# An MLP's two layers by Strassen's product in blocks of 256 pixels, inside a four-layer fp32 kernel

## The chip, the cores and the metric

One core of a Trainium2 chip; everything is fp32. The time is the device time of one execution in microseconds; one core, so it is that core's. A run quoted here is the median of its executions, with the lowest and highest in brackets.

## The reference, cut to what matters

Four image layers follow each other: a deformable attention with an MLP (layer 0), then three attention layers. Only the MLP at the end of layer 0 is changed. With B x H x W = 2 x 32 x 32 = 2048 pixels and C = 512 channels:

```python
xn2 = _bn(x, bn2_g, bn2_b)
h1 = jax.nn.gelu(jnp.einsum('bchw,oc->bohw', xn2, mlp_w1) + mlp_b1[None, :, None, None], approximate=False)
return x + jnp.einsum('bchw,oc->bohw', h1, mlp_w2) + mlp_b2[None, :, None, None]
# mlp_w1: 2048 x 512, mlp_w2: 512 x 2048
```

## The kernel before: the parts that matter

`w1` (4 chunks of 128 input channels x 2048 outputs) and `w2` (16 chunks x 512) lie in SBUF. A half image of 512 pixels is a block; `P` is 128, `CC` 4, `HID` 2048, `HALF` 512. `norm` is a generator that computes the next layer's group norm step by step between the MLP's groups.

```python
xn = normed(0, 0)
for b in range(B):
    for half in range(2):
        ...
        h1 = one.tile([P, HID // P, HALF], F32, name="hid")
        for m in range(HID // P):
            ph = ps.tile([P, HALF], F32, name="ph")
            for k in range(CC):
                nc.tensor.matmul(                                   # L991: first layer
                    ph, w1[:, k, m * P : (m + 1) * P], xn_now[:, k, :], start=(k == 0), stop=(k == CC - 1)
                )
            nc.scalar.activation(h1[:, m, :], ph, AF.Gelu, bias=col("mlp_b1", m))
            if b == 1 and m % 4 == 3:
                advance(norm)
        if (b, half) == (B - 1, 1):
            qkv1, proj1 = load_w(wa, "wa", [a["qkv1_w"], a["proj1_w"]])
        for m in range(CC):
            pp = ps.tile([P, HALF], F32, name="pp2")
            for k in range(HID // P):
                nc.tensor.matmul(                                   # L1002: second layer
                    pp, w2[:, k, m * P : (m + 1) * P], h1[:, k, :], start=(k == 0), stop=(k == HID // P - 1)
                )
            nc.vector.scalar_tensor_tensor(
                xs[b][:, m, n], pp, col("mlp_b2", m), xs[b][:, m, n], ALU.add, ALU.add
            )
            nc.sync.dma_start(out=x_d[b, m, :, n], in_=xs[b][:, m, n])
```

## Time and profile before

| | before |
|---|---|
| time, us | 3727.63 (3726.69 to 3728.03, the first 3 runs) |
| TensorE busy | 99% of 3725.8 us |
| MLP, first matmul to the next layer's first | 440.2 us (12%) |
| VectorE busy in one pair of MLP layers (110 us) | 2.8 us |
| pitch of a matmul record of 512 columns | 429.1 ns |

How to read it: TensorE (PE) works without a gap through the MLP, so the MLP's time is the number of its matmul records times their pitch, the time from one record's start to the next one's. A record is half of one fp32 matmul of the program. The lines behind the table are shown in the prediction below.

### The profile page before, as it was taken

To read this page: it belongs to the slowest core of one execution; us is meant where nothing else is said; L and a number is where in the kernel's file an instruction comes from. 1 tells how busy PE (TensorE), PEld (TensorE's weight loads), DVE (VectorE), ACT (ScalarE), POOL (GpSimd) and SP (SyncE) were. 2 spreads that over 40 slices of the span, in tenths; PEclk is the share of its full clock that TensorE was granted. 3 is DMA by queue.
4 is the path that set the end of the run, shared out by engine and by line. 5 is a ranking of instruction groups with operands and counts; after the bars stand their busy time and mean duration, and the time that the engine had idled before them with its cause. 6 is when DMAs were issued, how large, how long until landed. Compare 5 with 4: busy or idle time off the path is not lost.

```text
span 3725.8 us, 37390 instructions
## 1 busy us (share of the span) xinstructions
PE 3675.3 (99%) x15234; PEld 1342.1 (36%) x15234; DVE 2371.8 (64%) x2317; ACT 1586.4 (43%) x1940; POOL 478.6 (13%) x188
## 2 busy tenths in 40 slices
PE   9999999999999999999999999999999999999999
PEld 4333333333333333333333334444433333444443
DVE  6988998998996998998998960000036447030222
ACT  4655566565664566656656541100134234111111
POOL 1112122122121012121132210000001000000000
PEclk9999999999999999999999999999999999999999
DMA  4100012001010110010101001000100000000000
GB/s 149 24 15 14 18 24 62 17 20 18 18 23 12 13 23 18 18 24 12 24 18 22 18 2 51 9 34 12 57 1 1 1 1 0 14 0 0 6 29 24
DMA packets 96852, 78.42 MB, mean 21 GB/s; under 512 B 10656, under 2 KB 84768, under 8 KB 95904
## 3 DMA queue, kind: packets, MB, share of 16 engines
q1 hardware_dynamic: 96528, 75.41, 8.3%
q8 instruction: 123, 2.02, 0.2%
q14 instruction: 57, 0.47, 0.0%
q10 hardware_dynamic: 144, 0.52, 0.0%
HBM read 64.12 MB, written 10.75 MB: 20 GB/s over the span
## 4 chain that ended last, share of the span: by engine, by line
PE 93%; DVE 3%; ACT 3%; issue 0%; DMA 0%; POOL 0%; SPq 0%; DVEq 0%; POOLq 0%; ACTq 0%
PE z L443 44%; PE sim L465 6%; PE pw L135 6%; PE ph L991 6%; PE pp L1002 6%; PE pm L1026 5%; PE pmv L135 4%; PE score L1130 3%; PE score L135 3%; PE pv L1178 3%; PE ppr L1057 2%; PE pp L549 1%; ACT h L451 1%; DVE h L425 1%; DVE h L456 1%; PE pf L135 1%
## 5 line engine op out<-in xcount | busy, mean ns | idle before, releaser
L443 PE MATMUL z<-h,cpb_w 128*64 128x512 f32 x8192 | 1788.7, 594 | 28.5 <-ACT h L451 26.6
L451 ACT ACTIVATE h<-z,b2h 128x1024 f32<-128x1024 f32 x1024 | 1137.8, 1114 | 868.0 <-PE z L443 858.7
L425 DVE CUSTOM_DVE_ANT_1 h<-tab,tab 128x1024 f32<-128x1024 f32 x1024 | 1221.8, 1234 | 121.1 <-PE z L443 120.7
L443 PEld LDWEIGHTS z<-h,cpb_w 128*64 128x64 f32 x8192 | 575.6, 137 | 1208.9 <-issue 1107.5
L456 DVE SCALAR_TENSOR_TENSOR h<-h,turn,h 128x1024 f32<-128x1024 f32 x512 | 689.6, 1347 | 5.3 <-ACT h L451 5.3
L410 POOL TENSOR_SCALAR tab<-tab,pc 128x512 f32<-128x512 f32 x63 | 270.9, 4300 | 1576.3 <-DMA tab<-slog_d 1116.3
L1005 DVE SCALAR_TENSOR_TENSOR x<-pp,pc,x 128x512 f32<-128x512 f32 x16 | 12.0, 749 | 375.8 <-PE pp L1002 375.8
L465 PE MATMUL sim<-h,w 128*32 128x512 f32 x2048 | 234.3, 595 | 0.7 <-DVE h L456 0.7
L135 PE MATMUL pw<-p,vT 128*128 128x512 f32 x512 | 221.8, 593 | 1.3 <-DVE y L1236 1.3
L991 PE MATMUL ph<-xn,wa 128*128 128x512 f32 x512 | 220.9, 593 | 1.4 <-POOL xn L975 1.4
L1002 PE MATMUL pp<-hid,wb 128*128 128x512 f32 x512 | 220.4, 592 | 0.0
L1131 ACT ACTIVATE p<-score 128x1024 f32<-128x1024 f32 x144 | 139.5, 1021 | 156.8 <-PE score L1130 156.8
L1068 DVE TENSOR_TENSOR acc<-acc,p 128x2048 f32<-128x2048 f32 x56 | 129.6, 2315 | 105.1 <-ACT p L1131 57.8
L994 ACT ACTIVATE hid<-ph,pc 128x512 f32<-128x512 f32 x64 | 44.0, 687 | 332.6 <-PE ph L991 332.6
L953 POOL TENSOR_SCALAR hc<-x,sc,sh 128x1024 f32<-128x1024 f32 x16 | 29.0, 1822 | 902.3 <-DVE sh L949 870.1
L1070 DVE TENSOR_TENSOR acc<-p 128x2048 f32<-128x2048 f32 x12 | 27.5, 2291 | 182.2 <-ACT p L1265 108.8
L991 PEld LDWEIGHTS ph<-xn,wa 128*128 128x128 f32 x512 | 97.1, 190 | 123.2 <-issue 120.4
L1002 PEld LDWEIGHTS pp<-hid,wb 128*128 128x128 f32 x512 | 97.4, 190 | 122.4 <-issue 122.4
L135 PEld LDWEIGHTS pw<-p,vT 128*128 128x128 f32 x512 | 97.1, 190 | 122.5 <-issue 120.9
L411 POOL TENSOR_SCALAR tab<-tab,pc 128x512 f32<-128x512 f32 x63 | 131.1, 2081 | 16.3 <-DMA tab<-slog_d 16.2
L1130 PE MATMUL score<-q,k 64*128 64x512 f32 x512 | 127.2, 615 | 0.0
L1026 PE MATMUL pm<-hc,wa 128*64 128x512 f32 x512 | 122.5, 604 | 0.0
(217 smaller groups left out, 2044.5 us busy)
## 6 DMA issues: line engine op xcount, KB each, us to landing
tab<-slog_d SPq DMA_DIRECT2D x128, 256.0 KB, 6.3
wa<-in_qkv_w SPq DMA_DIRECT2D x8, 768.0 KB, 6.8
xt<-in_xt SPq DMA_DIRECT2D x8, 512.0 KB, 3.8
wa<-in_mlp_w SPq DMA_DIRECT2D x4, 1024.0 KB, 17.0
wb<-in_mlp_w SPq DMA_DIRECT2D x16, 256.0 KB, 5.4
x_d<-x SPq DMA_DIRECT2D x16, 256.0 KB, 2.0
out<-x SPq DMA_DIRECT2D x16, 256.0 KB, 2.0
wa<-in_proj_w SPq DMA_DIRECT2D x8, 256.0 KB, 9.0
```

The costliest lines, as they stand in the source:

```text
L135: nc.tensor.matmul(pm, w, m, start=(k == 0), stop=(k == len(pairs) - 1))
L410: engine.tensor_scalar(tabs[0], tabs[0], col("cpb_w1", 0), col("cpb_b1"), ALU.mult, ALU.add)
L425: nc.vector._custom_dve(TENSOR_ADD_SAT, out=h1, in0=tx[:, quad, ri, :].unsqueeze(1).to_broadcast([P, H, W]), in1=ty[:, quad, ri, :].unsque ...
L443: nc.tensor.matmul(z[point * 64 : point * 64 + 64, n], cpb_w2[:, part * 64 : part * 64 + 64], h1s[point][:, n], start=True, stop=True,)
L451: nc.scalar.activation(h2, z, AF.Relu, bias=b2h[:, part : part + 1])
L456: nc.vector.scalar_tensor_tensor(parts[0], parts[0], turn, parts[1], ALU.mult, ALU.add)
L465: nc.tensor.matmul(sim[quad * 32 : quad * 32 + 32, n], w3[:, lo : lo + 32], h2[:, n], start=(r == 0 and j < 4), stop=False,)
L991: nc.tensor.matmul(ph, w1[:, k, m * P : (m + 1) * P], xn_now[:, k, :], start=(k == 0), stop=(k == CC - 1))
L1002: nc.tensor.matmul(pp, w2[:, k, m * P : (m + 1) * P], h1[:, k, :], start=(k == 0), stop=(k == HID // P - 1))
L1026: nc.tensor.matmul(pm[at : at + wide], w[:, k, lo + at : lo + at + wide], h[k][:, n], start=(k == 0), stop=(k == CC - 1),)
L1130: nc.tensor.matmul(sc[:, part, :], ks[part][r, left[part]], qs[part][r, n], start=True, stop=True)
L1131: nc.scalar.activation(p[:, :, n], sc, AF.Exp, scale=scale)
```

## The change

The intent: TensorE is the bound and VectorE idle in the MLP, so multiply less and add more. Each layer's weights and pixels are split into halves; Strassen's scheme (in Winograd's form) gets the product of two 2 x 2 arrays of blocks from seven products instead of eight. The blocks are now 256 pixels, so a product streams 128 pixels. The sums on the weights' side are formed once, on VectorE, while block 0 is computed in the plain way; those on the pixels' side are formed for each block, and the seven products are combined on VectorE (with ScalarE copying product 1 out of PSUM). Condensed:

```diff
+            def lefts(w, name):                     # sums of the weights, once
...
+                def form(engine, cols):
+                    engine.tensor_tensor(t1[c], a21[c], a22[c], ALU.add)
+                    engine.tensor_tensor(t2[c], t1[c], a11[c], ALU.subtract)
+                    engine.tensor_tensor(a21[c], a11[c], a21[c], ALU.subtract)
+                    engine.tensor_tensor(t4[c], a12[c], t2[c], ALU.subtract)
+                return (a11, a12, t4, a22, t1, t2, a21), form
+            def rights(v, name):                    # the same for the pixels, by chunk (L1006 to L1009)
...
+            def products(left, right, cols, some, pms=None):
+                a, b = pms                          # two PSUM tiles, "pma" and "pmb", of 4 x 128 columns
+                at = {1: a[:, 0], 2: a[:, 1], 6: a[:, 2], 3: a[:, 3], 4: b[:, 0], 5: b[:, 1], 7: b[:, 2]}
+                for i in some:
+                    product(at[i], i, left, right, cols)
+            def combined(pms, p1, lower):
...
+                nc.vector.tensor_tensor(upper, a[:, 1:3], twice(p1), ALU.add)              # L1036
+                nc.vector.tensor_tensor(u, b[:, 1:3], twice(upper[:, 1]), ALU.add)         # L1037
+                nc.vector.tensor_tensor(lower, b[:, 0:2], twice(u[:, 1]), ALU.add)         # L1038
+                nc.vector.tensor_tensor(upper[:, 1], a[:, 3], u[:, 0], ALU.add)            # L1039
...
+            for blk in range(1, NBLK):
+                for c in range(MC + 1):             # MC = 8 groups of first-layer outputs
+                    if c < MC:
+                        pms = products(left1, right1, slice(c * P, (c + 1) * P), (1, 2, 6, 7, 5, 4, 3))
+                        p1 = first_of(pms)          # nc.scalar.copy, L1044
+                    if c:
+                        activated(c - 1, upper)     # Gelu of the lower half L1095, of the upper L1096
+                    if c < MC:
+                        upper = combined(pms, p1, hid[:, MC + c, :].rearrange("p (j n) -> p j n", j=2))
+                    if c:
+                        form_right2(slice(c - 1, c))
+                    if b == 1 and c % 4 == 3:
+                        advance(norm)
...
+                cols = [slice(c * P, (c + 1) * P) for c in range(2)]
+                both = [products(left2, right2, cols[c], (1, 2)) for c in range(2)]
+                for c in range(2):
+                    products(left2, right2, cols[c], (6, 7, 5, 4, 3), both[c])
+                    lower = two.tile([P, 2, PX], F32, name="lower")
+                    upper = combined(both[c], first_of(both[c]), lower)
+                    added(blk, 2 + c, lower.rearrange("p j n -> p (j n)"))
+                    added(blk, c, upper)
```

To make room, weights of a later layer (`g2`, `v2`, `vbias`) are loaded after the MLP instead of in its middle, and a buffer ring of that layer is split in two.

More of the change, by code (lines that the diff above doesn't have):

```diff
@@ L884, in general, with layers @@
             attend([(k[:DH], q[:DH])], 1.0, vT, [(m * P, P) for m in range(CC)], store)
-    def layers(f, g2, v2, t2_b, o2_b):
+    def layers(f, fold_d, t2_b, o2_b):
         f.enter_context(in_order(tc))
@@ L891, in layers @@
         keep = f.enter_context(tc.tile_pool(name="keep", bufs=1))
-        chan = f.enter_context(tc.tile_pool(name="chan", bufs=9))
+        chan = f.enter_context(tc.tile_pool(name="chan", bufs=4))
         ps_m = f.enter_context(tc.tile_pool(name="ps_m", bufs=2, space=PSUM))
@@ L898, in layers @@
             nc.sync.dma_start(out=vb, in_=a["vb"].rearrange("l (k p) -> p l k", p=P))
-        vbias = keep.tile([P, C], F32, name="vbias")
-        nc.sync.dma_start(out=vbias, in_=a["vb"][0].partition_broadcast(P))
         gb3 = keep.tile([P, CC], F32, name="gb3")
@@ L969, in layers, with blocks @@
             ps = mlp.enter_context(tc.tile_pool(name="mlp_ps", bufs=3, space=PSUM))
-            def normed(b, half):
-                n = slice(half * HALF, (half + 1) * HALF)
-                xn = two.tile([P, CC, HALF], F32, name="xn2")
+            BLK = 256
+            PX = BLK // 2
+            def blocks(v, k, n):
+                return [
+                    [v[:, i * k // 2 : (i + 1) * k // 2, j * n // 2 : (j + 1) * n // 2] for j in range(2)]
+                    for i in range(2)
+                ]
@@ new lines, in lefts @@
+            def lefts(w, name):
+                k, n = w.shape[1:]
+                (a11, a21), (a12, a22) = blocks(w, k, n)
+                t1, t2, t4 = [one.tile([P, k // 2, n // 2], F32, name=f"{name}s{i}") for i in (1, 2, 4)]
+                def form(engine, cols):
+                    c = (slice(None), slice(None), cols)
+                    engine.tensor_tensor(t1[c], a21[c], a22[c], ALU.add)
[3 more added lines that the diff above has]
+                return (a11, a12, t4, a22, t1, t2, a21), form
@@ new lines, in rights, with form @@
+            def rights(v, name):
+                k, n = v.shape[1:]
+                (b11, b12), (b21, b22) = blocks(v, k, n)
+                t1, t2, t4 = [one.tile([P, k // 2, n // 2], F32, name=f"{name}t{i}") for i in (1, 2, 4)]
+                def form(chunks):
+                    c = (slice(None), chunks, slice(None))
+                    nc.vector.tensor_tensor(t1[c], b12[c], b11[c], ALU.subtract)
+                    nc.vector.tensor_tensor(t2[c], b22[c], t1[c], ALU.subtract)
+                    nc.vector.tensor_tensor(b12[c], b22[c], b12[c], ALU.subtract)
+                    nc.vector.tensor_tensor(t4[c], b21[c], t2[c], ALU.subtract)
+                return (b11, b21, b22, t4, t1, t2, b12), form
@@ new lines, in product @@
+            def product(pm, i, left, right, cols):
+                l, r = left[i - 1], right[i - 1]
+                accumulate(pm, [(l[:, k, cols], r[:, k, :]) for k in range(l.shape[1])])
+            def products(left, right, cols, some, pms=None):
+                if pms is None:
+                    pms = [ps.tile([P, 4, PX], F32, name=f"pm{i}") for i in "ab"]
+                a, b = pms
+                at = {1: a[:, 0], 2: a[:, 1], 6: a[:, 2], 3: a[:, 3], 4: b[:, 0], 5: b[:, 1], 7: b[:, 2]}
+                for i in some:
+                    product(at[i], i, left, right, cols)
+                return pms
@@ new lines, in combined, with twice @@
+            def combined(pms, p1, lower):
+                a, b = pms
+                upper = two.tile([P, 2, PX], F32, name="upper")
+                u = two.tile([P, 2, PX], F32, name="u")
+                def twice(v):
+                    return v.unsqueeze(1).to_broadcast([P, 2, PX])
+                nc.vector.tensor_tensor(upper, a[:, 1:3], twice(p1), ALU.add)
+                nc.vector.tensor_tensor(u, b[:, 1:3], twice(upper[:, 1]), ALU.add)
+                nc.vector.tensor_tensor(lower, b[:, 0:2], twice(u[:, 1]), ALU.add)
+                nc.vector.tensor_tensor(upper[:, 1], a[:, 3], u[:, 0], ALU.add)
+                return upper.rearrange("p j n -> p (j n)")
@@ L974, in normed, with first_of @@
+            def first_of(pms):
+                p1 = two.tile([P, PX], F32, name="p1")
+                nc.scalar.copy(p1, pms[0][:, 0])
+                return p1
+            left1, form1 = lefts(w1, "w1")
+            left2, form2 = lefts(w2, "w2")
+            def normed(blk):
+                b, n = blk * BLK // HW, slice(blk * BLK % HW, blk * BLK % HW + BLK)
+                xn = one.tile([P, CC, BLK], F32, name="xn2")
                 for cc in range(CC):
@@ L978, in normed @@
                 return xn
-            xn = normed(0, 0)
-            for b in range(B):
-                for half in range(2):
-                    n = slice(half * HALF, (half + 1) * HALF)
-                    xn_now = xn
-                    if (b, half) != (B - 1, 1):
-                        xn = normed(*divmod(2 * b + half + 1, 2))
-                    h1 = one.tile([P, HID // P, HALF], F32, name="hid")
-                    for m in range(HID // P):
-                        ph = ps.tile([P, HALF], F32, name="ph")
-                        for k in range(CC):
-                            nc.tensor.matmul(
-                                ph, w1[:, k, m * P : (m + 1) * P], xn_now[:, k, :], start=(k == 0), stop=(k == CC - 1)
-                            )
-                        nc.scalar.activation(h1[:, m, :], ph, AF.Gelu, bias=col("mlp_b1", m))
-                        if b == 1 and m % 4 == 3:
-                            advance(norm)
-                    if (b, half) == (B - 1, 1):
-                        qkv1, proj1 = load_w(wa, "wa", [a["qkv1_w"], a["proj1_w"]])
-                    for m in range(CC):
-                        pp = ps.tile([P, HALF], F32, name="pp2")
-                        for k in range(HID // P):
-                            nc.tensor.matmul(
-                                pp, w2[:, k, m * P : (m + 1) * P], h1[:, k, :], start=(k == 0), stop=(k == HID // P - 1)
-                            )
-                        nc.vector.scalar_tensor_tensor(
-                            xs[b][:, m, n], pp, col("mlp_b2", m), xs[b][:, m, n], ALU.add, ALU.add
-                        )
-                        nc.sync.dma_start(out=x_d[b, m, :, n], in_=xs[b][:, m, n])
-                if b == 0:
-                    for w, j in ((g2, 0), (v2, 1)):
-                        nc.sync.dma_start(out=w, in_=fold_d[j])
@@ new lines, in normed_rights, with added @@
+            def normed_rights(blk):
+                right, form = rights(normed(blk), "xn")
+                form(slice(0, CC // 2))
+                return right
+            NBLK = B * HW // BLK
+            MC = HID // P // 2
+            def added(blk, m, src):
+                b, at = blk * BLK // HW, blk * BLK % HW
+                x = xs[b][:, m, at : at + BLK]
+                nc.vector.scalar_tensor_tensor(x, src, col("mlp_b2", m), x, ALU.add, ALU.add)
+                nc.sync.dma_start(out=x_d[b, m, :, at : at + BLK], in_=x)
@@ new lines, in layers @@
+            xn = normed(0)
+            hid = one.tile([P, HID // P, BLK], F32, name="hid")
+            for c in range(MC):
+                for m in (MC + c, c):
+                    pm = ps.tile([P, BLK], F32, name="pmp", tag="pma")
+                    accumulate(pm, [(w1[:, k, m * P : (m + 1) * P], xn[:, k, :]) for k in range(CC)])
+                    nc.scalar.activation(hid[:, m, :], pm, AF.Gelu, bias=col("mlp_b1", m))
+                form1(nc.vector, slice(c * P, (c + 1) * P))
+            right1 = normed_rights(1)
@@ new lines, in layers, with activated @@
+            for m in (2, 3, 0, 1):
+                pm = ps.tile([P, BLK], F32, name="pmp2", tag="pmb")
+                accumulate(pm, [(w2[:, k, m * P : (m + 1) * P], hid[:, k, :]) for k in range(HID // P)])
+                added(0, m, pm)
+                if m >= 2:
+                    form2(nc.vector, slice((m - 2) * P, (m - 1) * P))
+            for blk in range(1, NBLK):
+                b = blk * BLK // HW
+                hid = one.tile([P, HID // P, BLK], F32, name="hid")
+                right2, form_right2 = rights(hid, "hid")
+                def activated(c, upper):
+                    nc.scalar.activation(hid[:, MC + c, :], hid[:, MC + c, :], AF.Gelu, bias=col("mlp_b1", MC + c))
+                    nc.scalar.activation(hid[:, c, :], upper, AF.Gelu, bias=col("mlp_b1", c))
+                upper = None
+                for c in range(MC + 1):
[10 more added lines that the diff above has]
+                        advance(norm)
+                if blk + 1 < NBLK:
+                    right1 = normed_rights(blk + 1)
+                else:
+                    qkv1, proj1 = load_w(wa, "wa", [a["qkv1_w"], a["proj1_w"]])
+                cols = [slice(c * P, (c + 1) * P) for c in range(2)]
[6 more added lines that the diff above has]
+                    added(blk, c, upper)
@@ L1104, in layers @@
         wb_stack.close()
+        fold2 = f.enter_context(tc.tile_pool(name="fold2", bufs=1))
+        vbias = fold2.tile([P, C], F32, name="vbias")
+        nc.sync.dma_start(out=vbias, in_=a["vb"][0].partition_broadcast(P))
+        g2, v2 = [fold2.tile([P, CC, C], F32, name=name) for name in ("g2", "v2")]
+        for w, j in ((g2, 0), (v2, 1)):
+            nc.sync.dma_start(out=w, in_=fold_d[j])
+        outs = f.enter_context(tc.tile_pool(name="outs", bufs=5))
         vp = f.enter_context(tc.tile_pool(name="vp", bufs=1))
@@ L1191, in layers @@
                 if ls == 7:
-                    o = chan.tile([P, HW], F32, name="o", tag="chan")
+                    o = outs.tile([P, HW], F32, name="o")
                     nc.vector.tensor_copy(o, pv)
@@ L1328 @@
         w1 = layer0(l0, fold_d, t2_b, o2_b)
-    with tc.tile_pool(name="fold2", bufs=1) as pool, ExitStack() as fast:
-        g2, v2 = [pool.tile([P, CC, C], F32, name=name) for name in ("g2", "v2")]
-        layers(fast, g2, v2, t2_b, o2_b)
+    with ExitStack() as fast:
+        layers(fast, fold_d, t2_b, o2_b)
     bad = nc.values_load(flag[0:1, 0:1], min_val=0, max_val=P)
```

## The prediction

> **What bounds the kernel now.** I read the page first: TensorE (PE) is busy for 99% of the span at a granted clock of 0.9 or more in every slice, and the chain that ended last is 93% PE. So only what shortens PE's own work, or makes PE wait, can move the time.
>
> ```profile
> span 3725.8 us, 37390 instructions
> PE 3675.3 (99%) x15234; PEld 1342.1 (36%) x15234; DVE 2371.8 (64%) x2317; ACT 1586.4 (43%) x1940; POOL 478.6 (13%) x188
> PEclk9999999999999999999999999999999999999999
> PE 93%; DVE 3%; ACT 3%; issue 0%; DMA 0%; POOL 0%; SPq 0%; DVEq 0%; POOLq 0%; ACTq 0%
> ```
>
> Then the chain in order of time, from 2240 us on (start, length, what). The MLP is these eight stretches without a gap, alternating first layer (L991) and second (L1002).
>
> ```profile
> 2246.53 0.78 POOL xn L975
> 2247.31 0.35 issue
> 2247.66 55.17 PE ph L991 x128
> 2302.84 54.93 PE pp L1002 x128
> ...
> 2632.88 54.93 PE pp L1002 x128
> 2687.82 13.88 PE pm L1026 x64
> ```
>
> The MLP therefore takes 2687.82 - 2247.66 = 440.2 us, 12% of the span. One fp32 matmul of the program leaves two records (64 matmuls, 128 records), and 54.93/128 = 429.1 ns is the pitch of one record of 512 columns. The 592 ns that the groups show is a latency; records overlap, so I count pitches only.
>
> The busy time of each engine in the stretches of the first half block's two layers (us, PE, PEld, DVE, ACT, POOL) shows how empty the others are:
>
> ```profile
> 2247.70:2302.80 55.10, 55.10 (x129) 24.51 (x130) 0.57 (x1) 11.59 (x16) 4.84 (x7) 1.00 0.24 81
> 2302.80:2357.80 55.00, 55.00 (x130) 24.41 (x129) 2.25 (x3) 0.69 (x1) 3.01 (x4) 1.00 0.04 15
> ```
>
> VectorE (DVE) has room here, and the change spends it. The groups that price the new, smaller instructions are these (line, operation, shapes, count, busy, mean ns):
>
> ```profile
> L135 PE MATMUL pk<-wy,xt 128*128 128x128 f32 x128 | 16.4, 282 | 0.0
> L518 PE MATMUL pa<-cst,at 128*128 128x128 f32 x64 | 8.7, 279 | 0.0
> L252 DVE TENSOR_TENSOR cpb_w<-cpb_w,pw 128x128 f32<-128x128 f32 x1 | 0.3, 279 | 0.0
> L1044 DVE TENSOR_TENSOR vT<-pmv,vbias 128x512 f32<-128x512 f32 x16 | 11.1, 691 | 62.1 <-PE pmv L135 62.1
> L1068 DVE TENSOR_TENSOR acc<-acc,p 128x2048 f32<-128x2048 f32 x56 | 129.6, 2315 | 105.1 <-ACT p L1131 57.8 <-ACT p L1265 45.8
> L994 ACT ACTIVATE hid<-ph,pc 128x512 f32<-128x512 f32 x64 | 44.0, 687 | 332.6 <-PE ph L991 332.6
> L389 ACT COPY vbd<-pkv 128x128 f32<-128x128 f32 x8 | 2.2, 275 | 0.0
> L939 ACT ACT_TABLE_LOAD x4 | 5.1, 1283 | 0.1
> ```
>
> The decisive one is pk: 128-column fp32 matmuls with fresh 128x128 weights each, exactly the new kind. Its 16 records take 2.05 us from first start to last end; the first lasts 377 ns, some 100 ns more than the usual 275 because its weight load is exposed. So the pitch is (2.05 - 0.10 - 0.275)/15 = 111.7 ns; I use 111.5. All eight bursts look alike. The weight load (190 ns a record) stays hidden at this pitch.
>
> **What the Trainium skill says.** "TensorE: Matmul & The Clock Gate", Back-to-back issue gap and the part on 53.3 ns: a warm pitch of N/2.4 + 2.5 ns. The trace agrees at 512 columns if a record is two passes: 2x512/2.4 + 2.5 = 429.2 against 429.1. At 128 it would give 109.2; the transposes pa do that (8 records in 0.87 us of the chain), pk is at 111.5, and the measured pk decides. "VectorE: DVE Perf Modes", Mode 2x_2P: fp32 tensor_tensor stays at one element a cycle of 0.96 GHz, 1.04 ns a column; the trace agrees (2315 - 691)/1536 = 1.06. "SBUF — State Buffer", Who interferes with whom: VectorE and GpSimd share a port pair under a lock; the trace agrees in that one L425 instruction takes 3394 ns against a median of 1217 beside GpSimd work. In the MLP GpSimd has only a few short operations at block boundaries. I book nothing for it.
>
> **The change part by part.**
>
> Removed: all eight stretches, 440.2 us. Now there are eight blocks of 256 pixels, the first plain, seven by Strassen.
>
> Block 0, plain: 128 matmuls of 256 columns, 256 records at 2x256/2.4 + 2.5 = 215.8 ns (an estimate between the two measured widths) = 55.2 us, as much as half of an old pair. VectorE forms sums of the weights beside it: 8x4 operations of 256 columns and 2x4 of 1024. From the rows, an operation costs about 145 + 1.05 ns a column: 128 columns 279, 256 413, 1024 1220. That is 13.2 + 9.8 = 23 us under 55, each behind a matmul that has read the old block; hidden. w2 lands about 15 us after the MLP starts (transfer view) and is first needed at 27.
>
> Blocks 1 to 7: a layer was 64 matmuls of 256 columns; it is now 112 of 128 columns (8 groups x 7 products x 2 chunks, or 2 x 7 x 8), seven eighths of the column work. A block has 224 matmuls, 448 records x 111.5 = 49.95 us, where a plain one has 55.0. Seven: 349.7 us. PE work is then 404.9, 35.3 us less than now. The ideal 7/8 would save 48 us; the fixed cost of short matmuls takes the rest.
>
> Is VectorE fast enough? A group of the first layer lasts 28 x 111.5 = 3.12 us on PE. VectorE does three additions of 256 columns, one of 128, then four of 128 to form the second layer's right sides: 3x413 + 5x279 = 2.63 us, plus some 35 ns for each of about six dependent steps = 2.85 us, 91% of the group. ScalarE: one copy 0.27, two Gelus of 256 columns at about 0.47 (687 less 256 x 0.84) = 1.2 us. Both fit, barely for VectorE, and three PSUM buffers of each kind let PE run ahead. So PE still bounds within the layer.
>
> Where PE waits: between the layers. In the built program the copy of the first product waits for the last matmul of its group, so the whole combination starts when the group ends. Take the moment S at which PE would begin the second layer; the last group's results are there at S + 0.165 (275 less 111). Copy done S + 0.48; three additions with gaps S + 0.51, 0.96, 1.40 to 1.82; last addition to 2.10; Gelu of the lower half 1.85 to 2.32; of the upper to 2.83. PE's first product needs that upper half in its eighth chunk, at S + 14 x 0.1115 = 1.55. It waits **1.3 us** a block, 9.1 us for seven. The formed sums are needed only after four products (7.1 us) and are there by S + 4.
>
> In blocks 4 to 7 the next layer's norm is interleaved. Each of the first four steps puts 1.54 us (two statistics, one aggregate) on VectorE; with 0.3 us of slack a group, some 0.3 us is left at the boundary in three blocks, 1 us. The step with Ln and Exp costs two table loads of 1.28 us during which VectorE waits: about 3.3 us of delay in group 3 of the last block, 2.4 left at the boundary. Together 3.4 us.
>
> After the MLP: qkv1's weights (4 MB) are now loaded under 25 us instead of 55; they took about 11.5 us at 390 GB/s in the transfer view. g2, v2 and vbias load after the MLP; vbias has 14 us, the others hundreds. Fewer chan buffers delay the second norm's outputs, but by the built program's waits the first two are free one projection step (5.5 us) before they are read. I book 0.
>
> Sum: 404.9 + 9.1 + 3.4 = 417.4 us against 440.2: **22.8 us less**, 3727.6 - 22.8 = 3704.8, so 3705 us, 0.6% faster.
>
> **The rivals.**
> (A) VectorE becomes the bound in the first layer. At 3.4 us a group instead of 2.85 it would add (3.4 - 3.12) x 8 x 7 = 16 us: 3720. For it: 91% load, small operations, semaphores both ways with ScalarE. Against it: the op prices come from like operations, and the row with a PSUM operand (691 ns at 512 columns) lies on the same line as the one without (2315 at 2048).
> (B) The long stream of short matmuls runs slower than the bursts of 16: fetching or weight loading shows only over hundreds of records. At 122.8 ns all PE gain is gone (55.0/448), and the time would be about 3740. Against it: in the timeline, one-column matmuls with full weights (pb) run at about 101 ns a record (8 in 0.81 us), so weight loading is not quite at its limit.
> (C) PE reaches the 109.2 ns of the transposes and the boundaries overlap better (0.5 us): 3136 x 2.3 ns = 7.2 and 5.6 less: 3692.
> (D) A late load or buffer after the MLP stalls PE, 5 to 10 us: 3713. The margins above speak against it.
>
> **Range and chances.** Pitch uncertainty (109 to 113.5) is -8 to +6 us; boundaries 0.5 to 3 us each, -6 to +12; VectorE as in A. I take 3692 to 3720 for eight times in ten. Two per cent faster would need 3653, more than the ideal saving with no wait at all (48 us); two per cent slower 3802, which only a pitch over 140 ns gives.
>
> **What would show it.** In the changed kernel: 128-column matmul records 3136 in the MLP, pitch 111.5 inside a group; the MLP from first matmul to L1138's first in 417 us; a gap of about 1.3 us on PE released by ScalarE's Gelu (L1096) once a block, and no large gaps released by VectorE; VectorE near 90% busy in first-layer windows and a third in the second; time after the MLP unchanged at about 1038 us. It is wrong if the pitch differs, if PE waits for VectorE in every group, or if the stretch after the MLP grows.

## The result, and the profile after

| | before | changed |
|---|---|---|
| time, us | 3727.4 (3726.69 to 3728.03, 4 runs) | 3706.11 (3705.36 to 3712.39, 4 runs) |
| ratio | | 0.9947 [0.9929, 0.9964] |
| MLP, first matmul to the next layer's first | 440.2 | 417.4 |
| from there to the end | 1037.98 | 1038.21 |

A ratio is the mean time of one kernel's fast runs over that of the other's of the same rounds, so not quite the ratio of the medians quoted. The change is 21.3 us faster; predicted were 22.8 and 3705 us.

The profiled execution is the slowest of the four, 3712.39 us. Its excess lies outside the change: its MLP begins at 2254.89 us, where before it began at 2247.66. These 7.2 us are there by 220 us after the start, in code that the change doesn't touch. A later run of the same kernel (e9) has the MLP begin at 2248.9 and last 417.4 us again. I compare the MLP's duration from here on, since the start differs by up to 7 us from run to run.

The traces show what goes with that difference: the clock that TensorE was granted in the first 90 us. The two windows, of the kernel before and of the changed one (the number after POOL's busy time is the granted clock):

```profile
20.00:90.00 70.00, 66.24 (x252) 27.90 (x252) 49.23 (x83) 26.63 (x29) 7.39 (x5) 0.98 0.38 110
20.00:90.00 70.00, 64.67 (x222) 29.04 (x222) 43.30 (x77) 22.19 (x26) 5.61 (x3) 0.90 0.36 104
```

The thirteen traces fall into four groups by this clock: at 0.98 the MLP begins at 2247.7 to 2248.2 us, at 0.95 at 2248.8 to 2249.2, at 0.93 at 2251.6 to 2251.8, and at 0.90 at 2254.9. Why the clock differs there from run to run is not known.

The page of the changed kernel (busy us, share, instructions; then VectorE's busy tenths in 40 slices):

```profile
span 3710.5 us, 43026 instructions
PE 3649.9 (98%) x17602; PEld 1550.3 (42%) x17602; DVE 2557.3 (69%) x2905; ACT 1615.8 (44%) x2074; POOL 488.7 (13%) x204
DVE  5988998998996898998998873455346447030222
```

PE is busy for 25.4 us less with 2368 records more: shorter records, closer together. VectorE has taken up the work of seven products, and the MLP's slices (the 25th to the 29th) no longer show zeros.

The chain of the changed kernel in order of time, through block 0, one border between layers, the start of the second layers of two blocks in a row, and the last one (start, length, what):

```profile
2254.89 55.49 PE pmp L135 x256
...
2334.95 0.46 PE pma L135 x4
...
2335.49 0.28 ACT p L1044
...
2335.78 0.44 DVE upper L1036
...
2336.24 0.43 DVE u L1037
...
2336.70 0.43 DVE hid L1038
...
2337.16 0.51 ACT hid L1095
2337.67 0.41 ACT hid L1096
...
2338.12 7.63 PE pma L135 x66
2345.75 5.36 PE pmb L135 x48
...
2389.57 7.63 PE pma L135 x66
...
2648.58 7.63 PE pma L135 x66
...
2672.29 7.87 PE pm L1138 x35
```

What to see. Forty-eight records in 5.36 us are a pitch of 111.67 ns. Between PE's last record of the first layer and its resumption at 2338.12 the chain runs over ScalarE's copy, three dependent additions and two Gelus, each starting 0.02 us after the one before: it is a latency, and PE's own work beside it isn't enough to cover it. From one resumption to the next (2338.12, 2389.57; the next is 2441.03) a block takes 51.46 us, where its 448 records at 111.67 ns are 50.03.

What PE waited for in the MLP (engine line waited for: us in total, times, longest):

```profile
PE pma L135 <- ACT hid L1096: 8.5, 8, 1.9
PE pmp L135 <- POOL xn L1054: 1.4, 1, 1.4
```

Of the eight stops, blocks 1 to 6 have one each and the last block two. There is no wait for VectorE. The second line stood before too (POOL xn, 1.4). And VectorE's operations of one group, in the timeline (start, length, engine, line, operation; in brackets the idle time before it):

```profile
2332.66 0.42 DVE L1036 TENSOR_TENSOR upper<-pma,p 128x256 f32<-128x256 f32 x1 [0.66 <-ACT p L1044]
2333.11 0.42 DVE L1037 TENSOR_TENSOR u<-pmb,upper 128x256 f32<-128x256 f32 x1
2333.57 0.42 DVE L1038 TENSOR_TENSOR hid<-pmb,u 128x256 f32<-128x256 f32 x1
2333.91 0.28 DVE L1039 TENSOR_TENSOR upper<-pma,u 128x128 f32<-128x128 f32 x1
2334.11 0.28 DVE L1006 TENSOR_TENSOR hidt<-hid 128x128 f32<-128x128 f32 x1
2334.43 0.29 DVE L1007 TENSOR_TENSOR hidt<-hid,hidt 128x128 f32<-128x128 f32 x1
...
2334.84 0.28 DVE L1009 TENSOR_TENSOR hidt<-hid,hidt 128x128 f32<-128x128 f32 x1
```

The eight operations take 2.46 us, from 2332.66 to 2335.12, although their durations sum to 2.67: an operation that doesn't need the result of the one before starts before that one has ended (2333.91 to 2334.11 is 0.20 us, at 0.28 us each). VectorE then stands idle for 0.66 us until the next group's product 1 is copied.

### The profile page after: what moved, and what is told of

The parts are those of the page before. It is cut to its first block, busy times and chain, and to the rows that moved or that the text cites. A ratio compares the mean times of both kernels' runs of the same rounds, so it can differ in the third digit from the quotient of the medians.

```text
span 3710.5 us, 43026 instructions
## 1 busy us (share of the span) xinstructions
PE 3649.9 (98%) x17602; PEld 1550.3 (42%) x17602; DVE 2557.3 (69%) x2905; ACT 1615.8 (44%) x2074; POOL 488.7 (13%) x204
## 4 chain that ended last, share of the span: by engine, by line
PE 94%; ACT 3%; DVE 1%; issue 0%; DMA 0%; POOL 0%; SPq 0%; ACTq 0%; DVEq 0%; POOLq 0%
PE z L443 46%; PE sim L465 6%; PE pw L135 6%; PE pma L135 5%; PE pm L1138 5%; PE pmv L135 5%; PE pmb L135 4%; PE score L1249 3%; PE score L135 3%; PE pv L1297 3%; PE ppr L1169 2%; PE pp L549 2%; PE pmp L135 1%; ACT h L451 1%; PE pf L135 1%; PE pk L135 0%
## 5 line engine op out<-in xcount | busy, mean ns | idle before, releaser
L1044 ACT COPY p<-pma 128x128 f32<-128x128 f32 x70 | 18.6, 266 | 313.3 <-PE pma L135 313.3
L1036 DVE TENSOR_TENSOR upper<-pma,p 128x256 f32<-128x256 f32 x70 | 29.6, 422 | 172.8 <-ACT p L1044 172.7
L411 POOL TENSOR_SCALAR tab<-tab,pc 128x512 f32<-128x512 f32 x63 | 132.1, 2097 | 19.1 <-DMA tab<-slog_d 18.6
L465 PEld LDWEIGHTS sim<-h,w 128*32 128x32 f32 x2048 | 60.8, 109 | 155.8 <-issue 152.7
L1297 PE MATMUL pv<-p,vT 128*64 128x512 f32 x512 | 121.4, 595 | 0.0
L135 PE MATMUL score<-t,hc 128*128 128x512 f32 x256 | 110.2, 592 | 0.0
L1355 DVE TENSOR_TENSOR y<-pw,r 128x512 f32<-128x512 f32 x32 | 21.8, 682 | 115.9 <-PE pw L135 115.9
```

The source lines that it names most:

```text
L135: nc.tensor.matmul(pm, w, m, start=(k == 0), stop=(k == len(pairs) - 1))
L411: engine.tensor_scalar(tabs[1], tabs[1], col("cpb_w1", 1), 1.0, ALU.mult, ALU.mult)
L465: nc.tensor.matmul(sim[quad * 32 : quad * 32 + 32, n], w3[:, lo : lo + 32], h2[:, n], start=(r == 0 and j < 4), stop=False,)
L1297: nc.tensor.matmul(pv[part * 64 : part * 64 + 64, n], vT[:, ls, lo : lo + 64], lp[:, part, n], start=(ls == 0), stop=(ls == 7),)
```

## The experiments

Three batches, each with the kernel before on the same chip (nine runs each; medians 3727.82, 3727.49 and 3728.06 us). All gave the reference's result. "MLP" is the duration defined above, from the trace. The experiments ask three things: where the 22.8 us come from, whether the border between the layers is what keeps the rest away, and whether VectorE's and TensorE's prices are understood.

### e1: all eight blocks plain

The smaller blocks, the moved loads and the buffers stay; the seven products and all sums go. Condensed:

```diff
-            for c in range(MC + 1): ... products(...); combined(...); form_right2(...)
-            both = [products(left2, right2, cols[c], (1, 2)) ...]
+            for c in range(MC):
+                for m in (MC + c, c):
+                    pm = ps.tile([P, BLK], F32, name="pmp", tag="pma")
+                    accumulate(pm, [(w1[:, k, m * P : (m + 1) * P], xn[:, k, :]) for k in range(CC)])
+                    nc.scalar.activation(hid[:, m, :], pm, AF.Gelu, bias=col("mlp_b1", m))
+            for m in (2, 3, 0, 1): ...              # 16 plain matmuls each, in every block
```

> All eight blocks of 256 pixels by plain products, no sums, the moved loads and smaller buffers kept. Theory (the gain is PE's saved column work less a wait between the layers): the plain block 0 of the changed kernel took 55.5 us, so the MLP takes 8 x 55.4 = 443 us against 440.2 before, and the time is 3729 to 3731. Rival 1 (part of the gain comes from block size or from the moved buffers and loads): below 3722. If it is above 3735, the repacking costs something that Strassen had to pay for too.

Measured: 3730.43 us (3729.61 to 3733.21), ratio 1.0007 [0.9993, 1.002]; MLP 443.0. The rest of the change gains nothing; it costs 2.8 us in the MLP, since a layer of half blocks has twice as many records, and 443.0/2048 = 216.3 ns a record is over half of 429.1. So the whole gain is Strassen's: 443.0 - 417.4 = 25.6 us against this base.

### e2 and e3: one layer by Strassen, the other plain

Condensed:

```diff
e2 -            both = [products(left2, ...)]  +  for m in (2, 3, 0, 1): plain; form2, form_right2 dropped
e3 -            products(left1, ...), combined  +  plain groups as in e1; form1, normed_rights dropped
```

> Strassen in the first layer only, the second plain with 256 columns. Theory: a block takes 25.0 + 27.6 = 52.6 us. The plain second layer reaches its eighth chunk only at S + 14 x 0.2158 = 3.02 us, the upper half is there at S + 2.85, so there is no wait at the boundary in six blocks and about 1.5 us in the last: MLP 55.5 + 7 x 52.6 + 1.5 = 425 us, time 3712. Rival 2 (each layer gives half of the measured 21.3 us, the wait belongs to the first layer's sums as such): 3717.

> Strassen in the second layer only, the first plain. Theory: no combination stands between the layers, a Gelu of the last chunk ends at about S + 0.7 and the second layer needs it at S + 1.55, so no wait: MLP 55.5 + 7 x 52.6 = 424 us, time 3711. The gains of the two halves (15.4 and 16.4 us) then add to some 32 us, more than the 21.3 of both together; the difference is the wait that only both together have. Rival 2: 3717, the halves adding up to the whole.

Measured: e2 3713.84 us (3711.49 to 3716.1), 0.9961 [0.9948, 0.9975], MLP 424.4; e3 3713.57 (3710.84 to 3713.87), 0.9959 [0.9946, 0.9973], MLP 424.7. Against e1's plain 443.0 the layers save 18.6 and 18.3 us, together 36.9, while both at once save 25.6. The missing 11.3 us are what only both together have; block by block the changed kernel loses 11.7 to stops (below). In e2 the waits of PE in the MLP are only

```profile
PE pmp L135 <- POOL xn L1053: 1.4, 1, 1.4
```

and the same line stands alone in e3. The border costs only where a combined result is needed soon by a Strassen product: in e2 the late chunk is still the eighth of the second layer's first output, but the records before it have 256 columns and take about twice as long, so it is needed later; in e3 no combination stands before the Gelu.

### e4: the late chunk asked for later

The second layer's product 1 needs the last group's chunk as its eighth. Here both output groups run their first seven chunks, then their eighth.

```diff
-                both = [products(left2, right2, cols[c], (1, 2)) for c in range(2)]
+                both = [[ps.tile([P, 4, PX], F32, name=f"pm{i}") for i in "ab"] for c in range(2)]
+                last = MC - 1
+                for ks in (range(last), range(last, MC)):
+                    for c in range(2):
+                        for k in ks:
+                            nc.tensor.matmul(both[c][0][:, 0], left2[0][:, k, cols[c]], right2[0][:, k, :], start=(k == 0), stop=(k == last))
+                for c in range(2):
+                    products(left2, right2, cols[c], (2,), both[c])
```

> The changed kernel with the second layer's first products reordered: chunks 0 to 6 of the first product for both output chunks, then chunk 7 of both. Nothing else moves. Theory: PE needs the late upper half at S + 28 x 0.1117 = 3.1 us instead of 1.56, it is there at S + 2.85: the wait of 1.43 us a block goes in six blocks, and 1.5 of the last block's 3.2 remains: the wait of PE on ScalarE falls from 8.5 us to under 2, time 3696 (3694 to 3698). Rival 3 (the wait is a backlog of VectorE that PE meets elsewhere): another wait takes its place, time 3703 to 3706.

Measured: 3695.52 us (3694.84 to 3697.59), 0.9914 [0.9901, 0.9928]; MLP 408.2. The waits of e4's PE in the MLP:

```profile
...
PE pma L1122 <- ACT hid L1096: 0.9, 2, 0.5
```

No instruction was removed, only the order of sixteen matmuls, and 9.2 us of the MLP are gone. This shows the border's wait as the cause of that loss. The wait that is left, 0.9 us, is in the last block, where the norm's step with its table loads sits.

### e5 and e10: product 3 into the other PSUM tile

In the built program the copy of product 1 waits for the last matmul that writes its tile. That is product 3, the last of the group. In the other tile, the copy and the first addition start earlier.

```diff
-                at = {1: a[:, 0], 2: a[:, 1], 6: a[:, 2], 3: a[:, 3], 4: b[:, 0], 5: b[:, 1], 7: b[:, 2]}
+                at = {1: a[:, 0], 2: a[:, 1], 6: a[:, 2], 3: b[:, 3], 4: b[:, 0], 5: b[:, 1], 7: b[:, 2]}
-                nc.vector.tensor_tensor(upper[:, 1], a[:, 3], u[:, 0], ALU.add)
+                nc.vector.tensor_tensor(upper[:, 1], b[:, 3], u[:, 0], ALU.add)
```

> The changed kernel with the third product, the last one of a group, moved to the free quarter of the second PSUM tile; the first tile is then complete four products earlier, and the copy and the first addition no longer stand behind the group's end. Theory (the wait at the boundary is the length of the chain after the group): the chain loses the copy and one addition, the upper half is there at about S + 2.15 us instead of 2.83 and is needed at S + 1.56: the wait falls by 0.7 us in each of seven blocks, time 3701. Rival 3 (VectorE's backlog): no change, 3706.

Measured: 3705.08 us (3698.89 to 3705.49), 0.9932 [0.9918, 0.9945], four us over the expectation, in two groups: 3698.9 twice and 3705.1 to 3705.5 three times. MLP 413.8. The same kernel again, in the last batch (e10):

> The third product in the second tile once more; its times had two groups, 3699 and 3705. Theory: the MLP is 413.9 us again, 3.5 us less than the changed kernel's, and the mean time is 3 to 4 us below that of the changed kernel in the same rounds. If its MLP is 417 us, the earlier profile was chance.

Measured: 3703.15 us (3698.98 to 3705.68), 0.9934 [0.992, 0.9947]; MLP 412.5, and the PE waits, the same in both runs:

```profile
PE pma L135 <- ACT hid L1096: 4.1, 7, 2.0
...
```

The wait is halved, 4.1 us for 8.5, and the MLP is 3.6 to 4.9 us shorter; by the times, e10's mean is 3.6 us under that of the changed kernel in the same batch. So the place of product 3 is a part of the border's cost. The 1.3 us between the two MLPs are in the last block. PE waits 2.0 us there in both; then the chain shows, in e5,

```profile
2640.56 9.01 PE pma L135 x66
```

and in e10

```profile
2636.83 7.63 PE pma L135 x66
```

The windows over these records show e5's clock granted at 0.84, and e10's at 1.00, so e5 lost the clock after the stop: from 2640.07 to 2643.48 us it was granted at 0.50. The rest of the 6.5 us between these two profiled runs is 3.8 us before the MLP and 1.5 after it, and both go with the clock too: in the first 90 us it is 0.93 in e5 and 0.98 in e10, and e5 has another stretch of 3.4 us at 0.50 from 3121.3 us, e10 none. The two groups of times agree with this: e5's runs at 3698.9 us had a mean clock of 0.999, those at 3705 one of 0.997. Without the lost clock (e10) the MLP is 4.9 us shorter than the changed kernel's, 0.7 a block, which is what was expected.

### e6 and e11: e4, e5, and the norm's steps moved

Six of the norm's eight steps go from the first layer, where they delay the combinations, into the second, where VectorE has time; two stay.

```diff
 e4 and e5, and
-                    if b == 1 and c % 4 == 3:
+                    if blk in (4, 5) and c == 3:
                         advance(norm)
...
                     added(blk, c, upper)
+                    if 4 <= blk < NBLK - 1:
+                        advance(norm)
```

> Last chunk later, third product in the second tile, and the norm's steps of Ln and Exp moved from the last block's first layer into an earlier block's second layer. Theory: PE never waits in the MLP, 55.5 + 7 x 50.03 + 0.2 = 406 us, against 408.2 with the reordering alone; time 3693 to 3694. If it is below 3690, something else than waiting was removed; if above 3697, the norm's new place costs.

Measured: 3693.68 us (3693.2 to 3693.92), 0.9909 [0.9894, 0.9925]; MLP 406.1. Again, as e11:

> All three edits once more, beside the changed kernel in the same rounds. Theory: the MLP is 406 us again, 11.3 us less than the changed kernel's, and the time 3692 to 3700, 10 to 12 us below the changed kernel's.

Measured: 3693.36 us (3693.01 to 3693.83), 0.9905 [0.989, 0.9921]; MLP 406.1. In both, PE's only wait in the MLP is the 1.4 us ahead of its first matmul. At the border the timeline of e6 has no idle time in brackets, neither for the weight loads nor the matmuls (start, length, engine, line, operation):

```profile
2329.24 3.65 PEld L1122 LDWEIGHTS pma<-hid,wb 128*128 128x128 f32 x32
2329.35 3.74 PE L1122 MATMUL pma<-hid,wb 128*128 128x128 f32 x32
```

This is the best version, better than both kernels: 34 us under the kernel before, and 12.6 under the changed kernel of the same batch. An MLP of 55.49 + 7 x 50.03 = 405.7 us would have no loss at all; it has 406.1. What is left can only come from the pitch or from fewer records. The 2.1 us below e4 belong to e5's edit and the norm's move together; no run has only one of them added to e4.

### e7: two more additions a group on VectorE

This asks for VectorE's true price. Two spare independent additions of 256 columns go into every group of the first layer. At 2.85 us a group VectorE would be over PE's 3.12 and become the bound; at the 2.46 us of the trace, from the start of the first addition to the end of the last, it would be over by 0.14 us.

```diff
                     if c:
                         form_right2(slice(c - 1, c))
+                    for _ in range(2 if c < MC else 0):
+                        spare = two.tile([P, 2, PX], F32, name="spare")
+                        nc.vector.tensor_tensor(spare, right1[0], right1[0], ALU.add)
```

> The changed kernel with two spare additions of 256 columns on VectorE in each of the 56 first-layer groups (results unused). It asks how near VectorE was to being the bound. By the trace after, a group's VectorE work takes 2.46 us from start to end of 3.13; two more of about 0.4 us make 3.26: it falls 0.14 us a group behind, PSUM buffers hide that until the boundary, and each block waits some 1.1 us longer: 3713 to 3715. By the recorded prediction's price (2.85 us a group) it would be 3.7 us, 0.6 behind a group: 3735 to 3740. By busy time alone (70% of a group) nothing would change: 3706.

Measured: 3713.54 us (3712.11 to 3716.32), 0.9963 [0.9949, 0.9976]; MLP 427.5, 10.1 us more than in the changed kernel. The busy time of each engine over seven groups of the first layer (us, PE, PEld, DVE, ACT, POOL, then clock and DMA), of the changed kernel

```profile
2313.06:2334.50 21.44, 21.44 (x194) 21.44 (x194) 15.03 (x50) 6.68 (x19) 0.00 (x0) 1.00 0.01 2
```

and of e7

```profile
2307.00:2328.40 21.40, 21.40 (x194) 21.40 (x194) 18.97 (x62) 6.67 (x19) 0.00 (x0) 1.00 0.01 2
```

VectorE is busy 70% of the time in the first and 89% in the second, and PE works without a gap in both. The wait for the border's Gelu has grown to 12.6 us, and a single one of 0.4 for VectorE has come.

The time is the expected one, but not for the expected reason. PE's first 66 records after each border, in the chain of e7 (blocks 1 to 7; start, length):

```profile
2332.05 7.63 PE pma L135 x66
2383.51 7.63 PE pma L135 x66
2434.96 7.63 PE pma L135 x66
2487.49 9.18 PE pma L135 x66
2541.55 9.26 PE pma L135 x66
2594.63 7.63 PE pma L135 x66
2650.76 9.46 PE pma L135 x66
```

Blocks 1 to 3 follow each other after 51.46 us, as in the changed kernel: two more additions a group cost nothing there. Where VectorE works without a pause, it starts a group's ten operations every 3.05 us (its first addition at 2482.11 and 2485.16), still under PE's 3.13, so it does not fall behind; the time from start to end had counted the last addition to its end, though the next one starts earlier. What VectorE no longer has is time to make up for the norm's steps. The stops at 2487.49 and 2541.55, in the two blocks with the norm's statistics, are 2.1 us long instead of 1.0, and so is one in the last block. With the end of these three stops the clock was granted at 0.50 for 3.4, 3.4 and 6.8 us, and the records shown take 1.5, 1.6 and 1.8 us longer: 5.0 of the 10.1 us. So the price of 2.85 us is too high, the trace's 2.46 us is a little too high as well, and that the time fell into the expected 3713 to 3715 is luck.

### e8: the pitch by itself

After the MLP five bursts of 160 fp32 matmuls (320 records) run, with their weights' width and their columns varied.

```diff
+        for name, wide, n in (("pa128", P, 128), ("pb64", 64, 128), ("pc32", 32, 128), ("pd256", P, 256), ("pe64", P, 64)):
+            pm = ps_m.tile([P, HALF], F32, name=name, tag="mm")
+            for i in range(160):
+                nc.tensor.matmul(pm[:wide, :n], w2[:, i % 16, :wide], w2[:, i % 16, 256 : 256 + n], start=True, stop=True)
```

> The changed kernel with five bursts of 160 fp32 matmuls each after the MLP, results unused, to measure the pitch of a record by itself in streams longer than any queue. Theory: 128 weight columns x 128 moving: 111.6 ns; 256 moving: 215.8; 64 moving with 128 weight columns: about 101, the pace of weight loads. If the 2.4 ns over 109.2 come from the weight load, 64 and 32 weight columns with 128 moving run at 109.2; if they belong to the short matmul, at 111.6 as well.

Measured: 3915.93 us in one run. The chain of e8 (start, length, what), in the order of the loop:

```profile
2667.16 35.73 PE pa L1128 x320
2702.89 35.08 PE pb L1128 x320
2737.97 35.05 PE pc L1128 x320
2773.02 69.26 PE pd L1128 x320
2842.28 35.68 PE pe L1128 x320
```

Divided by 320: 111.7 ns with 128 weight columns and 128 pixels; 109.6 and 109.5 with 64 and 32 weight columns; 216.4 with 256 pixels; and 111.5 with 64 pixels. With narrow weights 128 columns cost 109.5 ns; with full ones 111.7, and halving the pixels changes that by 0.2 ns only. So with full fp32 weights a record of 64 columns costs as much as one of 128, about 111.6 ns; other widths were not measured in a long burst. That a width of the weights moves it and the pixels don't is what a limit by the weight load gives; that the load is the limit is read from these two facts, not seen directly. I had expected about 101 ns at 64 pixels, from eight-record bursts: wrong. For the change it means that halving the 256-pixel blocks would not pay: it would double the records at an unchanged pitch.

### e9: the changed kernel again

> The changed kernel once more, on the chip and in the rounds of the two below: some of its runs were 6 to 7 us slower, and the trace puts that into the first 215 us, which no change touches. Theory: times fall into two groups about 6 us apart (3700 to 3706 and 3710 to 3712 or the like), and the MLP of the profiled run is 417.4 us again whichever group it is in.

Measured: 3705.95 us (3705.6 to 3708.9), 0.9941 [0.9927, 0.9954]; MLP 417.4, wait 8.5 us. The MLP is the same to 0.1 us. The two groups of times 6 us apart that I had expected from the first four runs of this kernel (one of them 3712.39) are not confirmed here: only one of five runs is slower, by 3 us.

## Why the prediction was right, step by step

The time, 3706.1 for 3705, and the MLP's duration, 417.4 for 417.4, agree closer than the steps do. Some errors cancelled, so that the sum agrees to 0.1 us is luck.

- **PE's work.** Block 0: 55.49 us for 55.2. The pitch: 111.67 ns for 111.5, so 350.2 us for 349.7. Together 405.7 for 404.9. Taking the pitch from pk, not the formula's 109.2, was decisive: 3136 x 2.5 ns is 7.8 us. Rival C is out on the pitch, rival B on the long stream. One remark beside the sum did not hold: that the weight load stays hidden at this pitch. In e8 narrower weights bring the record from 111.7 to 109.5 ns.
- **The border.** With S = 2335.23, PE's first record of the second layer, the upper half's Gelu ends at 2338.06 = S + 2.83, as worked out, though most of the steps before it come 0.04 to 0.12 us later than worked out and the two Gelus overlap by 0.1. Fourteen records at the pitch bring PE to S + 1.56 for 1.55. PE resumes at S + 2.89, 1.33 us later. The block loses 51.46 - 50.03 = 1.43 us for 1.3, so 10.0 us for 9.1; the 0.1 us between the two is the first record after the stop, which takes 0.38 us in the timeline where others take 0.275. The waits view shows only 1.02 us there, since the last record before the stop still runs (0.16 us beyond its pitch) and the two records before the stop had come 0.14 us late (the fourteen take 1.86 us in the timeline where the pitch gives 1.73): the chunk that they need, the seventh, leaves its Gelu at 2336.55, just as PE arrives. The loss is read from block to block, not from the wait.
- **The norm.** In the last block the loss is 3.2 us, of which 1.7 over the usual 1.43, for 2.4. The 0.3 us each in blocks 4 to 6 did not show: 1.7 for 3.4. The smaller number fits the next point, VectorE's larger slack. But the 1.7 us are largely something that the prediction had booked at nothing, GpSimd beside VectorE: it had placed GpSimd's work at block boundaries only. GpSimd computes the norm's output `hc` from 2637.98 to 2643.09, and of VectorE's additions in the chain of that time two are long:

```profile
2639.60 1.00 DVE hidt L1007
...
2642.45 0.79 DVE hidt L1006
```

  They last 1.00 and 0.86 us from start to end, where they last 0.29 and 0.28 in the other groups: 1.3 us more. Both have two inputs in SBUF; the additions that read PSUM at that time keep their 0.42 us. From there to the border VectorE has no pause, so about 1.3 of the 1.7 us come from this (an estimate; no run takes it out alone). Six more traces with `hc` at this place (e4, e5, e7, e8, e9, e10) show the same; in e5 and e10 it is two additions of 1.17 us. If so, the norm's own share is some 0.4 us where 2.4 were predicted for this block, and GpSimd's 1.3 where nothing was.
- **VectorE's load** is the step that failed. I had put 2.85 us, 91% of a group; it is 2.46 us from the first to the last, 70% busy, and in the second layer 23% instead of a third. Five operations of 128 columns were counted at their full duration of 279 ns, and 35 ns were added for dependent steps. But independent ones follow each other after 200 ns, and a dependent step costs 20 to 40 ns. With 0.66 us of slack instead of 0.3 a group, VectorE makes up more of the norm's delay before the border. Rival A is thus further away than I thought: in e7 ten operations a group still leave blocks 1 to 3 unchanged.
- **After the MLP** 1038.2 us for 1038.0: rival D is out. Both traces have one stretch of 3.4 us at a clock of 0.50 there; four experiments with the moved loads that lack it (e4, e6, e10, e11) take 1036.2 to 1036.6.

The sum: 55.5 + 350.2 + 7 x 1.43 + 1.7 = 417.4. Against the prediction's 417.4, PE's work was +0.8, the border +0.9, the norm -1.7.

Shown by experiments: the gain is the seven products' (e1), each layer alone saves 18.6 or 18.3 us against e1 (e2, e3), what they lose together is the border's chain (e4, e5), and without it the MLP is at PE's work (e6). Left open: why TensorE's clock is granted differently in the first 90 us from run to run, and why some stops of PE cost the clock: in the last block after 1.9 us it was lost in e8 and kept in the changed kernel and e9, after 2.0 us lost in e5 and kept in e10, and after 2.1 us lost three times in e7.

## What to carry to other kernels

Price a short matmul by a burst of the same shape in the trace: with full fp32 weights, 64 columns cost as much as 128 here, so an algorithm with fewer multiplications yields less than its ratio. When an engine's work is cut by adding steps on others, look for the place where the next layer needs the last result: the latency of that chain, not the others' load, set the loss, and reordering sixteen matmuls took most of it away. Count operations of VectorE by their start-to-start times and separate dependent from independent ones. When a time agrees, look whether the stretches agree too, and at the granted clock in each: in e7 half of the extra time was a lost clock.

## What the Trainium skill lacked or had wrong

- "TensorE: Matmul & The Clock Gate", Back-to-back issue gap: its formula N/2.4 + 2.5, taken for two passes a record, fits fp32 with narrow weights (109.5 ns measured for 109.2) and at 512 columns (429.1 for 429.2). The section says that the formula counts too little at small N, because it leaves out the weight load, and too much at large N. With full fp32 weights the first is so, and the section has no figure for fp32: 111.7 ns a record at 128 columns and 111.5 at 64. The second does not show at 512 columns. At 256 columns the formula gives 215.8; measured were 216.4 in e8 and 216.8 in block 0.
- The same page, Part 1, ties the loss of the clock to an idle window of about 3.4 us. In e5 a stop of 2.0 us was followed by 3.4 us at a granted clock of 0.50; in e10 a stop of the same length left 1.00. The rule doesn't tell that so short a stop can cost the clock, and not always.
- "VectorE: DVE Perf Modes", The DRAIN you can't avoid, says that an operation starts when the pipe has emptied, and that one that isn't held starts earlier, without a figure. The runs show it: independent fp32 additions of 128 columns start 0.20 us apart at a duration of 0.28; dependent ones of 256 columns 0.45 us apart at 0.42.
- None of the pages cited tells how much more a stop of PE costs than its wait shows: 1.02 us shown at a border, 1.43 us lost, because the record before it ends 0.275 us after its start where its pitch is 0.112, the first one after it is 0.1 us longer, and two records before it were already 0.14 us late.
